# Sorting the second group's lists by one-hot matrix products, and layer 1's norm with ScalarE squares, in a two-layer sparse graph kernel

## The chip, the cores and the metric

One core of one Trainium2 chip runs the kernel. The metric is the device time of one execution in microseconds (us). The profile is of one execution; its engines are called PE (TensorE matmuls), PEld (TensorE weight loads), DVE (VectorE), ACT (ScalarE), POOL (GpSimd, which also issues the indirect DMAs) and SP (SyncE, which here only issues DMAs).

## The reference, cut to what matters

The input is x, 3327 x 512, and a sparse symmetric adjacency matrix adj with ones on its diagonal. Two residual layers follow each other:

```python
# layer 0: graph attention with 4 heads
feats  = einsum('nf,hfo->hno', x, W)
logits = leaky(e_self[:, :, None] + e_neigh[:, None, :], 0.2), -1e10 where adj == 0
out    = relu(softmax(logits) @ feats + b)
x      = layernorm(x + out)
# layer 1: two gated sums over the same neighbours
attn_a = sigmoid([adj @ x, x] @ Wa.T + ba);  attn_b likewise with Wb, bb
h      = x @ W_sa
e      = where(adj != 0, exp(-leaky(s_left[:, None] + s_right[None, :], 0.01)), 0)
x_a    = (e / (sum(e) + 1e-5)) @ h
x_b    = adj @ (x @ W_gcnb) + b_gcnb
x      = layernorm(x + sigmoid(attn_a * x_a + attn_b * x_b))
```

A row of adj has few ones, so both layers can be computed from lists of neighbours: a node's row of a table is fetched for each neighbour, weighted and summed.

## The kernel before, in words

Nodes are cut into 26 tiles of 128, in two groups: 12 tiles (the first group) and 14 (the second). The kernel runs in three stages, in an order written out by hand, and every engine executes its instructions in that order.

**Lists and features (0 to about 215 us).** adj is loaded in chunks; matmuls with powers of two (`make_codes`, L371) and the top-8 instructions of VectorE (`top8`, L69) turn each column into a list of neighbours. `features` (L344) makes the rows of `table0`. A node's list is a row of 32 words in the tile `st`: its number, 24 neighbours, its number within the group, and four scores. Within a group the nodes are then sorted by degree, so that a tile needs as many fetches as its longest list (`CAPS`, L26). `rank_b` (L464) computes each node's place in the order (`ranki`), and `sort` (L496) writes every tile's list rows to their places in DRAM by an indirect DMA (`scatter`, L143) and reads them back as `srt[g]`. The first group is sorted early, among the features; the second after the first three tiles' fetches have been issued (L809), on POOL's queue, with the reading back on SP's.

**Layer 0 (about 215 to 560 us).** A loop over the tiles (L828), in an order with long and short tiles mixed. `gather` (L592) fetches a tile's rows, one indirect DMA on POOL per neighbour slot, into buffers of up to 6 rows, of which there are 7 (`GB`); it is called three tiles ahead. `weigh_a` and `weigh_b` make the softmax weights on VectorE and ScalarE, `attend` (L748) scales the rows (two of three on VectorE, the third on ScalarE) and adds them up on TensorE by products with the identity. In iteration i the order on TensorE is: `columns2` of tile i-2 (needs a copy `xt` by ScalarE), the sums of tile i, the transposes of tile i-1 (`columns1`). VectorE's order is: the scaling of tile i, the residual sum and statistics of tile i-1, `columns3`, the weights of tile i+1. At i = 5 `climb(1, ...)` (L854) prepares the longest lists of the second group from `srt[1]`; the first fetch that needs `srt[1]` is of tile 23, called at i = 9. `publish` scales finished tiles and writes them to `table1`.

**Layer 1 (about 560 to 970 us).** A second loop (L1019) over the tiles: `gather` from `table1`; `weighted` (L958) makes the weighted sum on VectorE, one multiply-add (L967) per row; `plain_sum` (L973) makes the plain sum on TensorE, one product per row. To relieve TensorE, VectorE adds some rows in pairs (L969, chosen by `paired`, L937), and TensorE takes a pair as one row. `turn` transposes both sums, with copies on ScalarE, and `project` multiplies them with the two weight matrices. At the end of an iteration come L1059 (the residual sum of tile i-2), `weights_b` and `scaled_first` of the next tile (the latter one ScalarE instruction, L951, that starts the accumulator `sw`, which VectorE's first L967 needs), and `norm.add` with bn_stats and bn_aggr (L660, L661); at the end of each group of up to four tiles the same call also makes the inverse root (L669 to L676).

Of the kernel before, what the change touches and what calls it, by code (L numbers as in the profile page):

```python
# [8 lines left out]
F32 = mybir.dt.float32  # L9
AF = mybir.ActivationFunctionType  # L10
# [69 lines left out]
def sparse_pass(  # L80
# [59 lines left out]
    own1 = dram.tile([NG[1] * P, 2, ROW], F32, name="own1")  # L140
    lists = [dram.tile([n * P, LW], I32, name=f"lists{i}") for i, n in enumerate(NG)]

# [47 lines left out]


    p0 = tc.alloc_tile_pool(name="p0", bufs=1, side="right")
    psl = tc.alloc_tile_pool(name="psl", bufs=1, space=PSUM, side="right")
# [80 lines left out]
    nc.gpsimd.memset(all1, 1.0)  # L274
    st = p0.tile([P, NT, LW], I32, name="st")
    nc.gpsimd.memset(st, 0)
    nc.gpsimd.iota(st[:, :, 0], pattern=[[P, NT]], base=0, channel_multiplier=1)
    for g, n in enumerate(NG):
        nc.gpsimd.iota(st[:, T0[g] : T0[g] + n, S + 1], pattern=[[P, n]], base=0, channel_multiplier=1)

# [63 lines left out]
    def features(t):  # L344

        i = t * P // CH
        xc = xcs[i]
        o = t * P - chunks[i]
        pf = psf.tile([P, 2, 512], F32, tag="pf", name=f"pf{t}")
        for k, hh in ((k, hh) for hh in range(2) for k in range(KT)):  # L350
            nc.tensor.matmul(  # L351
                pf[:, hh, :HC], xc[:, k, o : o + P], w0[:, k, hh, :], start=(k == 0), stop=(k == KT - 1)
            )
        row = pj.tile([P, ROW], F32, tag="row", name=f"row{t}", bufs=4)
        nc.scalar.copy(row[:, 0:F].rearrange("p (h o) -> p h o", h=2), pf[:, :, 0 : F // 2])
        nc.scalar.activation(
            row[:, F : F + H], pf[:, 0, F // 2 : HC], AF.Identity, bias=pad if t == NT - 1 else 0.0
        )
        nc.scalar.copy(row[:, F + H : ROW], st[:, t, 0:1].to_broadcast([P, H]))
        nc.scalar.copy(st[:, t, S + 2 : S + 2 + H].bitcast(F32), pf[:, 1, F // 2 : HC])  # L360
        nc.gpsimd.dma_start(table0[t * P : (t + 1) * P, :], row)  # L361
# [65 lines left out]
    def pick(i):  # L427
# [21 lines left out]
        )  # L449
        nc.vector.tensor_scalar(st[:, t0 : t0 + nt, 1 : S + 1], some[:, :nt], float(N), None, ALU.add)  # L450

# [12 lines left out]
    def rank_b(g):  # L464
# [19 lines left out]
        ranks[g] = rk  # L484
        return ranki

# [8 lines left out]

    def sort(g, ranki, queue):  # L496

        put = lambda t: scatter(f"lists{g}", lists[g][:, :], ranki[:, t : t + 1], st[:, T0[g] + t, :])
        tasks.extend(lambda t=t: put(t) for t in range(NG[g]))
        tasks.append(lambda: queue.dma_start(srt[g], lists[g].rearrange("(t p) w -> p t w", p=P)))  # L500
        if g == 0:
            tasks.extend(lambda j=j: own_x(j) for j in range(NG[0]))

# [55 lines left out]
    for i in range(len(chunks)):  # L559
        make_codes(i)  # L560
        more(1)
        if i == NC0:
            rankis[0] = rank_b(0)
            sort(0, rankis[0], nc.gpsimd)
        turn_codes(i)
# [22 lines left out]
    gp = ctx.enter_context(tc.tile_pool(name="gp", bufs=1))  # L588
    m0 = ctx.enter_context(tc.tile_pool(name="m0", bufs=2))
    ps = ctx.enter_context(tc.tile_pool(name="ps", bufs=1, space=PSUM))  # L590
# [88 lines left out]
    class Norm:  # L679
# [6 lines left out]
        def add(self, k, y):  # L686
# [7 lines left out]
            done = (self.first, *rsqrt(self.pool, self.mv, n, f"{self.tag}{k}"))  # L694
            self.first, self.mv = k + 1, None
            return done

# [109 lines left out]
    for i in range(AHEAD):  # L807
        got[order0[i]] = gather(table0, order0[i])
    sort(1, rankis[1], nc.sync)  # L809
    later(len(tasks))  # L810
    nc.sync.dma_start(own1[:, 0, :], xo)
# [16 lines left out]
    for i in range(NT + 3):  # L828
# [22 lines left out]
        if 2 <= i < NT + 2:  # L851
            columns3(order0[i - 2])
        if i == 5:
            climb(1, m0, psx.tile([P, B * H], F32, tag="pcol", name="climb1", bufs=2)[:, : B + H])  # L854
# [10 lines left out]
    covered()  # L865
    psx.release()


# [68 lines left out]
    def paired(j):  # L937

        left = 4 + (CAPS[j] >= 13)
        got_ = set()  # L940
        for s0, n, g, _ in got[j]:
            for i in range(0, n - 1, 2):
                if left:
                    got_.add(s0 + i)
                    left -= 1
        return got_
# [62 lines left out]
    ends = {3, 7, 11, 15, 19, 22, 24, 25}  # L1009
    norm = Norm(m1, "n1", ends)  # L1010
    at_ = lambda i: order[i] if 0 <= i < NT else None
# [5 lines left out]
    scaled_first(at_(0))  # L1017
    ready = None
    for i in range(NT + 3):  # L1019
# [5 lines left out]
        if jp is not None:  # L1025
            sp = zs[jp, "sp"] = m1.tile([P, F], F32, tag="sp", name=f"sp{jp}")
            nc.scalar.activation(sp, plain[jp], AF.Copy, scale=gates[jp][:, 1:2])
            turn(jp, 0)
            turn(jp, 1)
        if j is not None:  # L1030
            plain_sum(j, False)
            weighted(j, 0)
        if jpp is not None:
            za = zs[jpp] = m1.tile([P, F], F32, tag="za", name=f"za{jpp}", bufs=GRP + 3)
# [22 lines left out]
        if jpp is not None:  # L1057
            za = zs[jpp]
            nc.vector.scalar_tensor_tensor(za, za, 0.5, row1(jpp)[:, 0:F], ALU.mult, ALU.add)  # L1059
        if j1 is not None:  # L1060
            weights_b(j1)
            scaled_first(j1)
        if jpp is not None:
            ready = norm.add(i - 2, zs[jpp])

# [451 lines left out]
```

## Time and profile before

| | |
|---|---|
| median of 3 runs | 970.43 us (966.85 to 974.26) |
| the profiled execution | 971.21 us, of which the span of the core is 969.50 us |
| mean granted TensorE clock | 0.907 of full |
| busy: PE, DVE, ACT, POOL | 804.4, 716.6, 278.2, 626.2 us |
| fetches of rows (L615) on POOL | 464, mean 1033 ns, 479.2 us busy |
| layer 0's sums (L763) on PE | 504 instructions, 230.8 us |
| layer 1's multiply-adds (L967) on DVE | 226, mean 749 ns, 169.3 us |
| layer 1's pair sums (L969) on DVE | 95, mean 692 ns, 65.7 us |
| scatters of lists (L145) | 26, median 971 ns, the second group's between 216 and 235 us |

An engine's busy time is a sum over stages with different limits. A group's "idle before" is time in which that engine stood still, with the instruction or transfer that ended the wait. A product of 32-bit numbers is two instructions on PE; their durations overlap, so a run of n such instructions in one line of the timeline gives the true rate: 24 of 128x512 took 10.46 us at full clock, 0.43 us each. POOL shows about 0.30 us of "issue" between two indirect DMAs even when it waits for nothing.

### The profile page before, as it was taken

The page shows a single profiled execution, that of the slowest core. Times are in us where ns is not written, and L with a number is a line of the kernel's source. Part 1 is how long each engine was busy: PE and PEld are TensorE (multiplying, and loading weights), DVE is VectorE, ACT ScalarE, POOL GpSimd, SP SyncE. Part 2 cuts the span into 40 slices and gives each one's busy share as a digit, 9 for nine tenths or more (in the row PEclk, how much of TensorE's full clock was granted, in tenths as well). Part 3 has the DMA queues.
Part 4 walks back from the last instruction along what each step waited for, and adds up shares of the span by engine and source line. Part 5 has one row for each costly group of instructions (what it writes and reads, how often), then busy time and mean ns, then how long its engine had stood idle before and what let it go on. Part 6 is the DMA issues. An engine that isn't in the chain of part 4 may idle for free.

```text
span 969.5 us, 10086 instructions
## 1 busy us (share of the span) xinstructions
PE 804.4 (83%) x2534; PEld 421.7 (43%) x2534; DVE 716.6 (74%) x2118; ACT 278.2 (29%) x820; POOL 626.2 (65%) x664
## 2 busy tenths in 40 slices
PE   4399887338897998989979839998989989899893
PEld 3277675114344444444434514444434434344341
DVE  4277878886465676667756738799989989989873
ACT  1022211004234343435333403223222232232231
POOL 6611144777777777677777367777777777777411
PEclk9699998557898999989998958999989999999997
DMA  9799999972988787787777257776676776666400
GB/s 321 289 353 376 399 332 382 360 205 76 401 312 247 218 271 225 257 282 231 231 227 232 92 166 192 195 187 188 189 197 196 187 195 183 187 185 188 129 33 36
DMA packets 74242, 221.87 MB, mean 229 GB/s; under 512 B 14944, under 2 KB 19216, under 8 KB 73280
## 3 DMA queue, kind: packets, MB, share of 16 engines
q0 software_dynamic: 47008, 153.87, 53.7%
q1 hardware_dynamic: 24512, 65.17, 17.7%
q10 hardware_dynamic: 2656, 2.10, 0.7%
q8 instruction: 23, 0.38, 0.2%
q14 instruction: 43, 0.35, 0.1%
HBM read 200.01 MB, written 28.55 MB: 236 GB/s over the span
## 4 chain that ended last, share of the span: by engine, by line
PE 45%; DVE 19%; DMA 12%; POOL 11%; issue 7%; ACT 4%; DVEq 0%; ACTq 0%; POOLq 0%
PE acc L763 21%; PE pf L351 9%; POOL g L615 7%; DMA g<-table,srt 7%; DVE sw L967 7%; DMA at<-in_adjB 3%; PE po L1007 3%; PE pcol L787 3%; PE acc L988 3%; PE acc L752 3%; DVE g L969 2%; ACT xt L784 1%; DMA a_row<-in_a_self 1%; PE x1t L780 1%; POOL sprod L321 1%
## 5 line engine op out<-in xcount | busy, mean ns | idle before, releaser
L615 POOL DMA_INDIRECT g<-table,srt x464 | 479.2, 1033 | 147.9 <-issue 121.9
L763 PE MATMUL acc<-g,ident 128*128 128x512 f32 x504 | 230.8, 614 | 1.4 <-DVE g L760 1.4
L967 DVE SCALAR_TENSOR_TENSOR sw<-g,e,sw 128x512 f32<-128x512 f32 x226 | 169.3, 749 | 12.7 <-ACT sw L951 8.5
L763 PEld LDWEIGHTS acc<-g,ident 128*128 128x128 f32 x504 | 100.4, 199 | 132.1 <-issue 101.1
L988 PE MATMUL acc<-g,ident 128*128 128x512 f32 x262 | 128.6, 618 | 24.9 <-DVE g L969 14.7
L351 PE MATMUL pf<-w,xc 128*128 128x260 f32 x416 | 102.2, 408 | 13.3 <-DVE w L291 13.3
L760 DVE TENSOR_TENSOR g<-g,w 128x512 f32<-128x512 f32 x176 | 110.5, 695 | 0.6
L1007 PE MATMUL po<-wg,sT 128*128 128x512 f32 x208 | 98.0, 616 | 0.0
L351 PEld LDWEIGHTS pf<-w,xc 128*128 128x128 f32 x416 | 83.6, 204 | 29.2 <-DVE w L291 14.1
L1007 PE MATMUL po<-wsa,sT 128*128 128x512 f32 x208 | 95.2, 601 | 0.3 <-ACT sT L1000 0.3
L758 ACT ACTIVATE g<-g,w 128x128 f32<-128x128 f32 x304 | 91.6, 389 | 0.7 <-DVE w L743 0.7
L988 PEld LDWEIGHTS acc<-g,ident 128*128 128x128 f32 x262 | 49.1, 193 | 95.8 <-issue 44.7
L361 POOL DMA_DIRECT2D table<-row x26 | 14.4, 555 | 85.4 <-ACT st L360 85.4
L969 DVE TENSOR_TENSOR g<-g 128x512 f32<-128x512 f32 x95 | 65.7, 692 | 3.3
L1037 ACT ACTIVATE za<-za 128x512 f32<-128x512 f32 x26 | 16.4, 631 | 170.8 <-DVE za L1035 170.8
L1007 PEld LDWEIGHTS po<-wg,sT 128*128 128x128 f32 x208 | 41.4, 200 | 52.2 <-issue 52.0
L1007 PEld LDWEIGHTS po<-wsa,sT 128*128 128x128 f32 x208 | 40.2, 194 | 51.3 <-issue 48.9
L145 POOL DMA_INDIRECT out<-za,srt x26 | 29.1, 1118 | 50.1 <-ACT za L1052 44.0
L787 PE MATMUL pcol<-v,xt 128*128 128x8 f32 x208 | 32.4, 283 | 33.1 <-ACT xt L784 33.1
L379 PE MATMUL pc<-at,pow 128*32 128x512 bf16 (+1 forms) x182 | 24.3, 436 | 33.2 <-DMA at<-in_adjB 19.4
L787 PEld LDWEIGHTS pcol<-v,xt 128*128 128x128 f32 x208 | 30.0, 222 | 38.8 <-ACT xt L784 38.6
L717 DVE TENSOR_TENSOR w<-g,srt 128x20 f32<-128x20 f32 (+3 forms) x55 | 9.7, 184 | 48.2 <-DMA g<-table,srt 46.9
(236 smaller groups left out, 933.3 us busy)
## 6 DMA issues: line engine op xcount, KB each, us to landing
at<-in_adjB SPq DMA_DIRECT2D x78, 512.0 KB, 11.4
g<-table,srt POOLq DMA_INDIRECT x464, 3.8
table<-row POOLq DMA_DIRECT2D x26, 260.0 KB, 6.2
xc<-in_xB SPq DMA_DIRECT2D x6, 1024.0 KB, 7.1
own<-in_xo SPq DMA_DIRECT2D x1, 3640.0 KB, 23.5
own<-table SPq DMA_DIRECT2D x1, 3640.0 KB, 42.0
at<-in_adjL SPq DMA_DIRECT2D x13, 256.0 KB, 13.2
table<-x1a SPq DMA_DIRECT2D x12, 260.0 KB, 5.7
```

Source lines behind the costliest of these rows:

```text
L145: put = nc.gpsimd.indirect_dma_start(out=dst, out_offset=bass.IndirectOffsetOnAxis(ap=rows, axis=0), in_=src, in_offset=None, bounds_check ...
L351: nc.tensor.matmul(pf[:, hh, :HC], xc[:, k, o : o + P], w0[:, k, hh, :], start=(k == 0), stop=(k == KT - 1))
L615: nc.gpsimd.indirect_dma_start(out=buf[:, q - q0, :], out_offset=None, in_=table[:, :], in_offset=bass.IndirectOffsetOnAxis(ap=srt[g][:, i ...
L752: nc.tensor.matmul(acc, ident, bias0, start=True, stop=False)
L758: nc.scalar.activation(gv[:, h, :], gv[:, h, :], AF.Copy, scale=w[:, s, h : h + 1])
L760: nc.vector.tensor_tensor(gv, gv, w[:, s, :].rearrange("p (h o) -> p h o", o=1).to_broadcast([P, H, FO]), ALU.mult)
L763: nc.tensor.matmul(acc, ident, buf[:, o + s - s0, 0:F], start=False, stop=(s == CAPS[j] and j not in T0))
L787: nc.tensor.matmul(pcol, xt1[:, k, :], v1[:, k, :], start=(k == 0), stop=(k == KT - 1))
L967: nc.vector.scalar_tensor_tensor(sw, g[:, i, 0:F], e[:, s : s + 1], sw, ALU.mult, ALU.add)
L969: nc.vector.tensor_add(g[:, i, 0:F], g[:, i - 1, 0:F], g[:, i, 0:F])
L988: nc.tensor.matmul(plain[j], to, row, start=(not sums_of_two and i == 0), stop=(sums_of_two and i == len(rows) - 1),)
L1007: nc.tensor.matmul(proj[j], sT[:, k, :], wt[:, k, :], start=(half + k == 0), stop=(half + k == KT))
```

## The change

1. `sort` is split. The first group is sorted as before (`sort0`). The second group's 14 scatters and the reading back are gone. In their place `sort1`, called at the end of iterations i = 1 to 7 of layer 0 for two tiles of lists each, makes two VectorE instructions per tile (`row_is`, 128 x 128, and `spread`, 128 x 14 x 30) and one product on TensorE that adds into one PSUM tile; after the last one, two VectorE copies take it to `srt[1]`. `row_is` and `spread` have two buffers each. `rank_b(1)` gets four more small VectorE instructions that split the place into tile and row. `climb(1, ...)` moves from i = 5 to i = 8.
2. The constants on POOL change: the list tile is split into `st0` and `st1` (the second in 32-bit floats), and a few index rows are added.
3. In layer 1 `Norm` is replaced by `SquareNorm`: L1059 gets an accumulator output with the row's sum, one small VectorE instruction makes the negative mean, and ScalarE squares the row with that as its bias, with the sum of squares as an accumulator output. The inverse root is made in the next iteration, after `weighted(j, 0)`.
4. `turn(jp, 1)` comes after `plain_sum(j, False)`.
5. `paired` takes up to five pairs of a tile's rows (six for the longest tiles), where it took four (five).
6. The pool `m0` is released ahead of layer 1.

```diff
-        nc.vector.tensor_scalar(st[:, t0 : t0 + nt, 1 : S + 1], some[:, :nt], float(N), None, ALU.add)
+        nc.vector.tensor_scalar(
+            (st0, st1)[g][:, l0 : l0 + nt, 1 : S + 1], some[:, :nt], float(N), None, ALU.add
+        )
...
+        ti = p0.tile([P, NM], I32, name="ti")
+        nc.vector.tensor_scalar(ti[:, :n], ranki[:, :n], 7, None, ALU.logical_shift_right)
+        nc.vector.tensor_scalar(ranki[:, :n], ranki[:, :n], P - 1, None, ALU.bitwise_and)
+        to = ls.tile([P, 2, NM], F32, name="to")
+        nc.vector.tensor_copy(to[:, 0, :n], ti[:, :n])
+        nc.vector.tensor_copy(to[:, 1, :n], ranki[:, :n])
+        return to
...
+    def sort1(to, t0, t1):
+        n = NG[1]
+        if t0 == 0:
+            in_place.append(ps.tile([P, KT * P], F32, tag="pt", name="sorted1")[:, : n * W1])
+        for t in range(t0, t1):
+            row_is = ls.tile([P, P], F32, tag="row_is", name=f"row_is{t}", bufs=2)
+            nc.vector.tensor_scalar(row_is, columns, to[:, 1, t : t + 1], None, ALU.is_equal)
+            spread = ls.tile([P, n, W1], F32, tag="spread", name=f"spread{t}", bufs=2)
+            nc.vector.scalar_tensor_tensor(
+                spread, tiles_.to_broadcast([P, n, W1]), to[:, 0, t : t + 1],
+                st1[:, t : t + 1, :].to_broadcast([P, n, W1]), ALU.is_equal, ALU.mult,
+            )
+            nc.tensor.matmul(
+                in_place[0], row_is, spread.rearrange("p t w -> p (t w)"), start=(t == 0), stop=(t == n - 1)
+            )
+        if t1 == n:
+            by_tile = in_place[0].rearrange("p (t w) -> p t w", t=n)
+            nc.vector.tensor_copy(srt[1][:, :, : S + 2], by_tile[:, :, : S + 2])
+            nc.vector.tensor_copy(srt[1][:, :, S + 2 : W1].bitcast(F32), by_tile[:, :, S + 2 :])
...
+    class SquareNorm:
...
+        def add(self, k, y):
+            i = k - self.first
+            less_mean = self.of[:, 0, i : i + 1]
+            nc.vector.tensor_scalar(less_mean, less_mean, -1.0 / F, None, ALU.mult)
+            square = self.pool.tile([P, F], BF16, tag="square", name=f"square{self.tag}{k}", bufs=1)
+            nc.scalar.activation(square, y, AF.Square, bias=less_mean, accum_out=self.of[:, 1, i : i + 1])
+            return k in self.ends
...
-    sort(1, rankis[1], nc.sync)
-    later(len(tasks))
...
-        if i == 5:
+        if 0 < i <= 7:
+            sort1(rankis[1], 2 * i - 2, 2 * i)
+        if i == 8:
             climb(1, m0, psx.tile([P, B * H], F32, tag="pcol", name="climb1", bufs=2)[:, : B + H])
...
-        left = 4 + (CAPS[j] >= 13)
+        left = 5 + (CAPS[j] >= 13)
...
             turn(jp, 0)
+        if j is not None:
+            plain_sum(j, False)
+        if jp is not None:
             turn(jp, 1)
         if j is not None:
-            plain_sum(j, False)
             weighted(j, 0)
+        if full:
+            ready = norm.finish(i - 3)
...
-            nc.vector.scalar_tensor_tensor(za, za, 0.5, row1(jpp)[:, 0:F], ALU.mult, ALU.add)
+            nc.vector.scalar_tensor_tensor(
+                za, za, 0.5, row1(jpp)[:, 0:F], ALU.mult, ALU.add, accum_out=norm.total(i - 2)
+            )
...
-        if jpp is not None:
-            ready = norm.add(i - 2, zs[jpp])
+        full = jpp is not None and norm.add(i - 2, zs[jpp])
```

`SquareNorm.finish` makes the same chain of small instructions as L669 to L676, from the sums of squares.

## The prediction, made before the changed kernel was run

> **What bounds the kernel now.** I read the windows view first, one row per stage, its columns being the window, the busy time and count of PE, PEld, DVE, ACT and POOL, then granted PE clock, DMA share and GB/s:
>
> ```profile
> 300.00:350.00 50.00, 42.05 (x128) 21.63 (x127) 35.29 (x109) 22.18 (x73) 38.12 (x40) 0.93 0.79 231
> 850.00:900.00 50.00, 49.74 (x140) 23.53 (x139) 46.58 (x107) 13.35 (x33) 39.34 (x35) 1.00 0.67 188
> ```
>
> In layer 0 PE is busiest, and POOL is full too: 40 instructions with 0.30 us of issue each make 38.1 + 12 = 50 us. In layer 1 PE, DVE and POOL all look full. So the timeline of each must say who waits for whom. POOL first, around the second group's sort:
>
> ```profile
> 214.99 0.95 POOL L624 DMA_INDIRECT g<-table,ids  x1 [0.30 <-DVE v1sum L823]
> 216.25 1.00 POOL L145 DMA_INDIRECT lists<-st,ranki  x1 [0.30 <-DVE w L729]
> ...
> 233.99 0.97 POOL L145 DMA_INDIRECT lists<-st,ranki  x1 [0.30 <-DVE w L729]
> 235.26 0.99 POOL L615 DMA_INDIRECT g<-table,srt  x1 [0.30 <-issue]
> ```
>
> The wrong line to trust would be the releaser's name: every gap is 0.30, so POOL waits for nothing. The 14 scatters hold the fetches of the fourth tile (i = 3) back from 216.25 to 235.26: 19.0 us. Who pays is seen on PE:
>
> ```profile
> 254.27 0.60 PE L780 MATMUL x1t<-ident,x1a 128*128 128x128 f32 x4
> ...
> 259.58 1.88 PE L787 MATMUL pcol<-v,xt 128*128 128x8 f32 x8 [4.71 <-ACT xt L784]
> ...
> 277.06 1.06 PE L787 MATMUL pcol<-v,xt 128*128 128x8 f32 x8 [0.73 <-ACT xt L784]
> ...
> 302.28 0.29 PE L547 MATMUL climb<-of,to_row 128*128 128x14 f32 x2
> 308.33 1.87 PE L787 MATMUL pcol<-v,xt 128*128 128x8 f32 x8 [5.76 <-ACT xt L784]
> ```
>
> A normal tile has a gap of 0.73 us ahead of L787. Two are long: 4.71 (DVE waited for the fourth tile's fetch, and ScalarE's copy stood behind those weights) and 5.76 (DVE sat 9.50 us in front of `climb` at i = 5; then weights, four publishes of 2.92 us together on ScalarE, and only then the copy). After both the same eight products take 1.87 instead of 1.06. From 312 to 404 PE has no other gap over 0.73 but one of 2.50, while a tile's last fetch lands 12 us or so ahead of its sum (at i = 9 POOL ends at 329.8, 3.8 us to landing by the page, the sum begins at 347.3): PE bounds, POOL doesn't. From 395 POOL bounds, but its restart at 395.15, after a wait of 4.25, comes when L843 (394.20 to 394.88) has read the own rows out of a buffer, and L843 follows PE. So PE's position near i = 13 sets the end of layer 0.
>
> In layer 1 the waits view of DVE from 640 to 925 lists three waits, 11.0 us in all, one of them this:
>
> ```profile
> DVE sw L967 <- ACT sw L951: 5.9, 7, 1.7
> ```
>
> DVE is never idle for PE's sums, and only 1.3 us for a fetch. It bounds, until short tiles leave PE alone on the chain from 919 to 954. The end of an iteration on DVE and ACT:
>
> ```profile
> 818.24 0.52 DVE L932 TENSOR_SCALAR e<-e,gate 128x11 f32<-128x11 f32 x1
> 818.44 0.69 DVE L660 BATCH_NORM_STATS2 st<-za 128x6 f32<-128x512 f32 x1
> 819.16 0.18 DVE L661 BATCH_NORM_AGGREGATE mvn<-st 128x2 f32<-128x6 f32 x1
> 819.55 1.54 DVE L967 SCALAR_TENSOR_TENSOR sw<-g,e,sw 128x512 f32<-128x512 f32 x2 [0.20 <-ACT sw L951]
> ...
> 818.79 0.72 ACT L951 ACTIVATE sw<-x1b,e 128x512 f32<-128x512 f32 x1 [1.22 <-DVE e L932]
> ```
>
> The statistics lie between L932 and L967, exactly where DVE must wait for L951 anyway (818.79 + 0.72 = 819.51). At the iteration's end before this one it is the same: L951 ends at 806.83, L967 starts at 806.87.
>
> **What the Trainium skill says.** "TensorE: Matmul & The Clock Gate", Part 1 (the HAM clock gate): about an idle window of 3.4 us halves PE's clock, and about as much work restores it. The trace agrees: 1.88 against 1.06 after gaps of 3.39 us and more. "VectorE: DVE Perf Modes", "Two Vector instructions with no wait between them": an operation with an accumulator output is two instructions. DVE has none in this trace; ScalarE's read of its accumulator at L909 takes 0.19 us. "Vector Engine (DVE) Microarchitecture Reference", section 7: a scalar-tensor-tensor with two SBUF sources that aren't bf16 halves its throughput, with no port left for the accumulator's readback. Without an accumulator the trace contradicts a halving: L1059 has such sources and takes 0.68, as L843 does from PSUM.
>
> **The change, part by part.**
>
> *Constants and features.* POOL ends its constants at 4.7 and waits 6.29 for a transfer; a few index rows more (0.13 to 0.38 each) fit there. The features' ScalarE copies keep their size. 0.
>
> *Rank.* Four more DVE instructions at 0.2 each (as L483 with its gap) between L483 and the first weights: on the path, +0.8.
>
> *The 14 scatters and SP's reading.* POOL -19.0, but limited by seven buffers: the fourth tile's second buffer is free only when tile 11's sum ends (225.1). Even so its 13 fetches at 1.26 end near 236 (eight of them after 226), and later ones stay ahead of PE. SP's two `own1` copies, which stood behind the reading back at 236.49, go early, beside the lists stage; the three tiles fetched there land 8 us or more ahead of use (third tile: 219.2, used 227.3). 0 but for the gap that goes.
>
> *The products of `sort1`.* 128x420: 0.43 x 420/512 = 0.35 an instruction, two a product, two products: 1.4 us of PE per iteration, seven times. From i = 2 to 6 they cover the 0.73 gap: net 0.7. Their DVE work, per tile 0.2 (as L437's 96 elements, 0.18) and 0.6 (L458: 0.52 for 350, with 1.05 ns an element from there to 512), 1.7 an iteration with gaps, lies where DVE is ahead of PE; 0. Two buffers each let DVE wait for the products before last, done by then.
>
> *The two hand-overs.* At i = 7 the copies to `srt[1]` wait for PE's last product, and weights, ScalarE's exp, casts and the copy `xt` queue behind them, PE behind that: 0.5 (L474: 350 from PSUM in 0.52) + 0.2 + 1.1 of weights + 0.24 + 0.4 + 0.56 = 3.0, with latency 3.1. At i = 8 `climb` does it again without the publishes: 5.76 - 2.92 = 2.9. The fetch that needs `srt[1]` (tile 23) waits for a buffer until the sum of i = 8 in any case.
>
> Ledger of PE until i = 9, in us: rank +0.8; i = 1: +1.4; i = 2: -4.71 - 3.1 (clock: 0.82 on L787, 0.95 on L752, 12.53 instead of 11.2 on the sum) + 1.4 = -6.4; i = 3, 4, 6: +2.1; i = 5: -5.76 - 2.7 (clock likewise) - 0.29 + 1.4 = -7.35; i = 7: +1.4 + 3.1 - 0.73 = +3.8; i = 8: +0.29 + 2.9 - 0.73 = +2.45. Sum -3.2, before the clock. The gap of 2.50 at 386.70 cost 1.5 (14.41 for 30 instructions, 12.9 at full clock), that of 3.39 at 416.76 cost 3.1. Between them I take 2.4 for each new gap: **layer 0 +1.6**, bounds -3.2 (none) and +3.0 (3.1 each).
>
> *ScalarE's squares.* Removed: 0.87 of DVE per tile, hidden behind L951: 0, except at one of the longest tiles, where L967 waits for L661 (-0.7). Added on DVE: the accumulator's read in L1059, ahead of L932, on the path. Likeliest 0.15, between 0.06 and ScalarE's 0.19; upper bound L1059 at half rate, +0.53. From i = 6 to 23 DVE bounds: 18 x 0.15 = +2.7. Before i = 6 fetches bound (DVE waited 4.83 for one at 626.5). `less_mean` (0.16) hides behind L951. The square comes after L951 on ScalarE, some 0.9 with its read; behind it queue `sp` and both copies of `turn`. Moving `turn(jp, 1)` behind at least one row (0.86 on PE) covers `sp`; project's wait stays about 0. The inverse root keeps its 2.3 us of DVE, elsewhere. End: square, read and `less_mean` (about 1.3) for 0.92 of statistics: +0.5.
>
> *Fifth pair.* By the list lengths only five tiles (lengths 11, 11, 12, 14, 14) have one more pair. DVE +0.65 each: +3.2. PE -0.86 each, not bounding there: 0.
>
> *`m0`'s release.* The next pool waits for readers done by 561.5; its first use that matters waits for a fetch until 573. 0.
>
> **Layer 1: +2.7 + 3.2 - 0.7 + 0.5 = +5.7.** Total +7.3 against the profiled run's own 971.2: 978.5. The median of runs lies 0.8 below that run, so I say **978**.
>
> **Rivals.** *Slow accumulator:* L1059 at half rate. One mechanism at one place, +0.53 in place of 0.15 in 18 iterations, +6.8, and 0.4 at the end: 985; with both clocks cold 986. For it: the skill's sentence. Against: L1059's 0.68 now. It decides from L1059 over about 0.95 us. *DVE relieved:* if L951's cover were not the limit, 18 x 0.65 = 11.7 would go (0.87 less `less_mean`), and with the clock warm (layer 0 at -3.2) the time is 971.2 - 3.2 + 5.7 - 11.7 - 0.8 = 961; if a hand-over is hidden too, 958. The 806.83 and 806.87 speak against it. *Table loads:* if the square belonged to another table set, two loads of 1.28 (row L355) per tile would stand in front of L951's successors, 26 x 2.6 = 66 us, hidden in part: 1000 or more. Unlikely. *POOL was the bound:* 19 us off, 952; the landings 12 us ahead of use exclude most of it.
>
> **How the numbers follow.** About 1% (9.7 us) is what a measurement can tell from no change. The likeliest case has 0.6: its own range is 970 to 984, and the part over 980.1, with what queues behind the new waits and isn't priced, is 0.2. The slow accumulator 0.2, DVE relieved or POOL's bound 0.15 (0.1 under 960.7), table loads and the rest 0.05, slower. So faster 0.10, same 0.45, slower 0.45. The range 966 to 990 leaves out most of the relieved case and table loads.
>
> **What would show it.** Gap ahead of L787's like near 255 gone, and a third fetch buffer's wait on PE in its place; two gaps of about 3 us at i = 7 and 8, with the eight products at 1.9 after them if the clock fell; L967 still starting 0.04 after ScalarE's `sw`, DVE idle 0.5 ahead of it; L1059 and its read under 0.9; 100 pair sums. Wrong if L967 starts earlier after L932 than now, or PE has no gaps at i = 7 and 8.

## The result, and the profile after

| | before | after |
|---|---|---|
| median of 12 runs each | 970.5 us (966.85 to 974.26) | 969.3 us (967.27 to 976.42) |
| ratio, 95% interval | | 0.9997 (0.9981 to 1.0013) |
| the profiled execution, its span | 971.21, 969.5 us | 967.27, 965.2 us |
| busy: PE, DVE, ACT, POOL | 804.4, 716.6, 278.2, 626.2 us | 800.9, 712.6, 297.7, 611.7 us |

No difference can be measured, where 978 was forecast. Here and below, a ratio and its interval leave out runs more than 1.5% above the fastest of the same kernel, while a median takes in all runs. The two windows shown of before read so after the change (window, busy time and count of PE, PEld, DVE, ACT and POOL, granted PE clock, DMA share, GB/s):

```profile
300.00:350.00 50.00, 44.40 (x126) 21.76 (x125) 30.94 (x101) 18.31 (x59) 32.78 (x34) 0.93 0.69 197
850.00:900.00 50.00, 47.47 (x127) 21.36 (x126) 45.73 (x105) 12.82 (x34) 39.05 (x36) 1.00 0.68 190
```

The stages differ in place by a few us, so these lines give only the picture: POOL is no longer full in this stretch of layer 0 (32.8 us and 34 times 0.30 of issue make 43), and nothing looks relieved in layer 1. The timelines say more. POOL, where the scatters were:

```profile
214.56 0.95 POOL L676 DMA_INDIRECT g<-table,ids  x1 [0.30 <-issue]
215.82 0.95 POOL L667 DMA_INDIRECT g<-table,srt  x1 [0.30 <-issue]
...
225.97 0.95 POOL L667 DMA_INDIRECT g<-table,srt  x1 [3.83 <-PE acc L855]
...
235.06 0.95 POOL L667 DMA_INDIRECT g<-table,srt  x1 [0.30 <-issue]
```

The fourth tile's fetches start at 215.82, 19.4 us earlier. After five of them POOL waits 3.83 us for PE to free a buffer, which the prediction had said, and the eighth after that ends at 236.0. PE, near the first place where it had stood still, and at the two new ones:

```profile
255.11 1.58 PE L548 MATMUL sorted<-spread,row_is 128*128 128x420 f32 x4
256.52 0.95 PE L879 MATMUL pcol<-v,xt 128*128 128x8 f32 x8
...
321.18 1.58 PE L548 MATMUL sorted<-spread,row_is 128*128 128x420 f32 x4
325.48 1.06 PE L879 MATMUL pcol<-v,xt 128*128 128x8 f32 x8 [2.72 <-ACT xt L876]
...
327.34 9.59 PE L855 MATMUL acc<-g,ident 128*128 128x512 f32 x18
...
337.19 0.29 PE L599 MATMUL climb<-of,to_row 128*128 128x14 f32 x2
340.36 1.11 PE L879 MATMUL pcol<-v,xt 128*128 128x8 f32 x8 [2.88 <-ACT xt L876]
```

At 256.52 there is no gap where 4.71 was: the fourth tile's fetches no longer come late, and the sort's products (1.4 us) fill what a normal tile has left, 0.73. At the ends of iterations i = 7 and 8, ahead of the next tile's products, are the two gaps that were forecast at 3.1 and 2.9. DVE stands in front of both hand-overs:

```profile
322.80 0.54 DVE L553 CAST srt<-sorted 128x364 int32<-128x364 f32 x1 [9.71 <-PE sorted L548]
...
337.52 0.17 DVE L600 TENSOR_TENSOR of<-climb,step_of 128x10 f32<-128x10 f32 x1 [3.75 <-PE climb L599]
```

In layer 1, the end of an iteration on DVE, then on ACT:

```profile
813.53 0.68 DVE L1156 SCALAR_TENSOR_TENSOR za<-za,x1b 128x512 f32<-128x512 f32 x1
814.14 0.08 DVE L1156 DVE_READ_ACCUMULATOR za<-za,x1b 128x1 f32 x1
814.14 0.15 DVE L1022 TENSOR_SCALAR gate<-gate 128x1 f32<-128x1 f32 x1
...
814.52 0.51 DVE L1025 TENSOR_SCALAR e<-e,gate 128x11 f32<-128x11 f32 x1
814.72 0.31 DVE L768 TENSOR_SCALAR ofn<-ofn 128x1 f32<-128x1 f32 x1
815.82 1.54 DVE L1060 SCALAR_TENSOR_TENSOR sw<-g,e,sw 128x512 f32<-128x512 f32 x2 [0.79 <-ACT sw L1044]
```

```profile
815.06 0.72 ACT L1044 ACTIVATE sw<-x1b,e 128x512 f32<-128x512 f32 x1 [1.21 <-DVE ofn L768]
815.69 0.71 ACT L770 ACTIVATE squaren<-za,ofn 128x512 bf16<-128x512 f32 x1
816.30 0.19 ACT L770 ACTIVATION_READ_ACCUMULATOR squaren<-za,ofn 128x1 f32 x1
816.40 0.17 ACT L984 COPY e<-x1a 128x1 f32<-128x1 f32 x1
```

And the same instruction without accumulator, on DVE in the kernel before:

```profile
817.26 0.68 DVE L1059 SCALAR_TENSOR_TENSOR za<-za,x1b 128x512 f32<-128x512 f32 x1
817.86 0.14 DVE L929 TENSOR_SCALAR gate<-gate 128x1 f32<-128x1 f32 x1
```

From its start to the next instruction's: 0.61 us with the accumulator, 0.60 without. The read of 0.08 overlaps. DVE's 0.87 of statistics are gone, and it now stands 0.79 idle in front of the first multiply-add, which starts 0.04 after ScalarE's `sw` (815.06 + 0.72), as before. DVE's waits from 637 to 917 show the same as a sum (us, times, longest), where before has 5.9 us in 7 waits in the same window:

```profile
DVE sw L1060 <- ACT sw L1044: 19.0, 18, 2.4
```

### The profile page after: what moved, and what is told of

Same layout as the page of the kernel before. It is cut to its first block, busy times and chain, and to the rows that moved or that the text cites. A ratio compares the mean times of both kernels' runs of the same rounds, so it can differ in the third digit from the quotient of the medians.

```text
span 965.2 us, 10206 instructions
## 1 busy us (share of the span) xinstructions
PE 800.9 (83%) x2552; PEld 418.7 (43%) x2552; DVE 712.6 (74%) x2157; ACT 297.7 (31%) x872; POOL 611.7 (63%) x654
## 4 chain that ended last, share of the span: by engine, by line
PE 58%; DVE 12%; DMA 11%; POOL 10%; issue 5%; ACT 4%; DVEq 0%; ACTq 0%; POOLq 0%
PE acc L855 20%; PE po L1100 11%; PE pf L369 9%; PE acc L1081 7%; POOL g L667 7%; DMA g<-table,srt 6%; DVE sw L1060 4%; DMA at<-in_adjB 3%; PE pcol L879 3%; PE acc L844 3%; DVE g L1062 2%; PE pt L1091 2%; ACT za L1149 1%; DMA a_row<-in_a_self 1%; ACT xt L876 1%
## 5 line engine op out<-in xcount | busy, mean ns | idle before, releaser
L855 PE MATMUL acc<-g,ident 128*128 128x512 f32 x504 | 230.1, 613 | 1.6 <-DVE g L852 1.6
L855 PEld LDWEIGHTS acc<-g,ident 128*128 128x128 f32 x504 | 99.8, 198 | 131.1 <-issue 99.5
L1081 PE MATMUL acc<-g,ident 128*128 128x512 f32 x252 | 123.2, 615 | 21.9 <-DVE g L1062 12.1
L1100 PE MATMUL po<-wg,sT 128*128 128x512 f32 x208 | 94.5, 597 | 0.0
L1081 PEld LDWEIGHTS acc<-g,ident 128*128 128x128 f32 x252 | 47.3, 194 | 90.3 <-issue 41.1
L1062 DVE TENSOR_TENSOR g<-g 128x512 f32<-128x512 f32 x100 | 69.2, 692 | 3.5
L397 PE MATMUL pc<-at,pow 128*32 128x512 bf16 (+1 forms) x182 | 24.4, 438 | 32.7 <-DMA at<-in_adjB 19.4
L879 PE MATMUL pcol<-v,xt 128*128 128x8 f32 x208 | 29.5, 269 | 25.1 <-ACT xt L876 25.1
L1093 ACT COPY sT<-pt 128x512 f32<-128x512 f32 x52 | 30.2, 582 | 55.3 <-PE pt L1091 55.1
L876 ACT COPY xt<-x1t 128x512 f32<-128x512 f32 x26 | 15.2, 583 | 97.8 <-PE x1t L872 97.8
## 6 DMA issues: line engine op xcount, KB each, us to landing
own<-in_xo SPq DMA_DIRECT2D x1, 3640.0 KB, 33.9
```

The costliest lines, as they stand in the source:

```text
L855: nc.tensor.matmul(acc, ident, buf[:, o + s - s0, 0:F], start=False, stop=(s == CAPS[j] and j not in T0))
L879: nc.tensor.matmul(pcol, xt1[:, k, :], v1[:, k, :], start=(k == 0), stop=(k == KT - 1))
L1062: nc.vector.tensor_add(g[:, i, 0:F], g[:, i - 1, 0:F], g[:, i, 0:F])
L1081: nc.tensor.matmul(plain[j], to, row, start=(not sums_of_two and i == 0), stop=(sums_of_two and i == len(rows) - 1),)
L1093: nc.scalar.copy(sT, pt)
L1100: nc.tensor.matmul(proj[j], sT[:, k, :], wt[:, k, :], start=(half + k == 0), stop=(half + k == KT))
```

## The experiments

To compare single executions, four stretches are used, all from the timelines:

- **A** runs from POOL's first fetch to the end of PE's sum of i = 7.
- **B** runs on to the end of the sum of i = 9.
- **C** runs on to the end of the last sum of layer 0.
- **D** lies in layer 1. It runs from the end of DVE's wait for a fetch near 623 to the end of its wait for `po` (PE's projection) near 942; in old_turn_3 that is the one that ends at 948.78.

The ends of D in before, in after and in four_pairs, on DVE:

```profile
626.52 0.23 DVE L902 TENSOR_SCALAR e<-g,x1b 128x3 f32<-128x3 f32 x1 [4.83 <-DMA g<-table,srt]
945.53 0.75 DVE L1035 SCALAR_TENSOR_TENSOR za<-bias_g,gate,po 128x512 f32<-128x512 f32 x1 [4.35 <-PE po L1007]
```

```profile
623.12 0.23 DVE L995 TENSOR_SCALAR e<-g,x1b 128x3 f32<-128x3 f32 x1 [3.27 <-DMA g<-table,srt]
941.93 0.75 DVE L1132 SCALAR_TENSOR_TENSOR za<-bias_g,gate,po 128x512 f32<-128x512 f32 x1 [5.14 <-PE po L1100]
```

```profile
625.64 0.23 DVE L995 TENSOR_SCALAR e<-g,x1b 128x3 f32<-128x3 f32 x1 [5.03 <-DMA g<-table,srt]
942.26 0.75 DVE L1132 SCALAR_TENSOR_TENSOR za<-bias_g,gate,po 128x512 f32<-128x512 f32 x1 [4.78 <-PE po L1100]
```

From D is taken what one wait, that of a tile with long lists for `to_rows`, has over 0.9 us. It is 3.2 us in before and 0.9 in sort_only, whose layer 1 is the same code. The eight products in front of it on PE say why. They took 5.99 us in before and 3.68 in sort_only, and that is the whole difference: PE ran slower there in one execution than in the other (3.68 in five of the ten executions below, 5.38 to 6.53 in before, old_turn_3, late_copies, both_3 and both_four).

```profile
722.13 5.99 PE L1007 MATMUL po<-wg,sT 128*128 128x512 f32 x8
```

```profile
722.68 3.68 PE L1100 MATMUL po<-wg,sT 128*128 128x512 f32 x8
```

Without this correction D is 319.0 in before, 321.8 in old_turn_3, and 320.6, 315.8 and 313.1 in late_copies, both_3 and both_four; in the others it changes nothing. All in us:

| kernel | A | B | C | D | time, ratio to before |
|---|---|---|---|---|---|
| before | 154.5 | 21.8 | 197.4 | 316.7 | |
| after | 141.9 | 30.9 | 197.8 | 318.8 | 0.9997 (0.9981 to 1.0013) |
| sort_only | 141.8 | 33.9 | 198.2 | 316.6 | 968.3; 0.9989 (0.9969 to 1.0010) |
| l1_only | 152.6 | 21.8 | 198.0 | 318.8 | 972.5; 1.0033 (1.0015 to 1.0051) |
| four_pairs | 143.6 | 30.9 | 197.5 | 316.6 | 967.0; 0.9990 (0.9970 to 1.0010) |
| late_copies | 141.9 | 22.8 | 199.1 | 318.0 | 961.4; 0.9925 (0.9905 to 0.9945) |
| bn_norm_3 | 142.6 | 33.9 | 199.1 | 318.3 | one execution, 974.3 |
| old_turn_3 | 143.1 | 30.9 | 197.8 | 320.3 | one execution, 974.1 |
| both_3 | 146.3 | 22.8 | 199.0 | 312.5 | 957.7; 0.9885 (0.9861 to 0.9909) |
| both_four | 142.4 | 24.5 | 197.8 | 310.3 | 955.6; 0.9862 (0.9837 to 0.9887) |

The four kernels from sort_only to late_copies ran on one chip, where the kernel before took 969.0 (median); both_3 and both_four on another, where it took 968.3; bn_norm_3 and old_turn_3 on a third, with 972.7 in one execution. What lies outside the four stretches doesn't differ by kernel, but it scatters: POOL's first fetch comes between 178.6 and 182.2 us in these ten executions, and from C's end to D's start are 72.7 to 74.2 us.

### sort_only and l1_only: each half of the change alone

sort_only is after with this taken back in layer 1 (and the order of the transposes with it); l1_only is before with it put in (cut; the accumulator output and `finish` go with `Norm` and `SquareNorm`):

```diff
-        left = 5 + (CAPS[j] >= 13)
+        left = 4 + (CAPS[j] >= 13)
-    norm = SquareNorm(m1, "n1", ends)
+    norm = Norm(m1, "n1", ends)
```

> After, with the statistics, the order of the transposes and the four pairs of the kernel before in layer 1: only the second group's lists and their products are changed. Theory A (the two new gaps of 2.7 and 2.9 us on PE cost 1.9 each in clock, not 2.4, and the gap that goes at i = 2 takes a colder stretch with it): PE ends the sum of i = 9 some 3 us earlier than before, layer 0 ends 2.5 to 3.5 earlier, and the time is 967 to 968 us (-3). Theory B (the prediction's ledger of layer 0 holds, and something else offsets it): layer 0 +1.6, 972 us. Theory C (the two kernels' profiled executions differ by chance): layer 0 within 1 us of before, 970.

> Before, with layer 1 of the kernel after (squares on ScalarE, fifth pair, order of the transposes). Theory A (the accumulator's read is free, 0.01 an iteration; the fifth pair costs 0.5 to 0.8 on each of five tiles; about as much comes back at tiles where DVE waited for PE's rows): from the start of layer 1's fetches to PE's last sum within 1 us of before (377.9 us), the time 969 to 971. Theory B (the prediction's terms hold in a layer 1 that starts as before): layer 1 +5.7, the time 976. Theory C (all of the profiled gain is layer 1's): 967.

No theory has both of its numbers right. The lists' half took 968.3 against 969.0, nothing that can be told from zero; the layer's half was slower by 0.33%, 3.2 us, with an interval from 1.5 to 4.9. Layer 0 as a whole (A, B and C) has 373.9 in sort_only and 373.7 in before, which is theory C's "within 1 us". Its A is as short as after's, but B is 3.0 us longer, with the same code. PE's timeline of sort_only says why:

```profile
327.15 1.88 PE L879 MATMUL pcol<-v,xt 128*128 128x8 f32 x8 [2.72 <-ACT xt L876]
...
343.35 1.72 PE L879 MATMUL pcol<-v,xt 128*128 128x8 f32 x8 [2.88 <-ACT xt L876]
...
346.77 9.69 PE L855 MATMUL acc<-g,ident 128*128 128x512 f32 x18
```

The gaps are 2.72 and 2.88 to the digit as in after, but here the eight products take 1.88 and 1.72 where after had 1.06 and 1.11, and the second sum 9.69 where after had 8.62. The same gap costs one execution more clock than another. So a single profile doesn't settle layer 0 to better than 3 us.

### four_pairs, bn_norm and old_turn: the three parts of layer 1

four_pairs is after with one line undone:

```diff
-        left = 5 + (CAPS[j] >= 13)
+        left = 4 + (CAPS[j] >= 13)
```

> After with four pairs of rows (five for tiles of 13 and more) as before: 95 pair sums for 100, and PE has one product more on each of five tiles. Theory A1 (DVE bounds on those tiles, and each pair's 0.65 us is on the path): layer 1 shorter by 2.5 to 3.3 us than in after, time -3. Theory A2 (PE bounds there as much as DVE, since DVE then waits for PE's rows): layer 1 within 1 us of after or longer by up to 4 us (five products of 0.86).

D is 316.6 against 318.8: the five pairs cost 2.2 us in all, 0.44 each of the 0.65 that DVE spends on one. (The same code scatters by less: 318.8, 318.8 and 318.0 in after, l1_only and late_copies, 316.7 and 316.6 in before and sort_only.) By D theory A1 comes nearest, a little below its range; the time, 967.0, doesn't contradict it. With four pairs, D is what it is in before and sort_only (316.7 and 316.6). So the squares and the order of the transposes together cost nothing and bring nothing that D can show.

Whether they cancel was asked of two more kernels, each after with one thing undone (bn_norm is cut as above):

```diff
# bn_norm
-    norm = SquareNorm(m1, "n1", ends)
+    norm = Norm(m1, "n1", ends)
# old_turn
-        if j is not None:
-            plain_sum(j, False)
-        if jp is not None:
             turn(jp, 1)
         if j is not None:
+            plain_sum(j, False)
             weighted(j, 0)
```

> The kernel of bn_norm once more, one look, for a chip without the long waits. From DVE's wait for a fetch near 623 to its wait for PE's last projection but one (less what the tile-0 wait for `to_rows` has over 0.9 us): theory A (the accumulator's read is free and the statistics lie in the wait for `sw`) 318.8 plus or minus 0.6 as after; prediction's terms 316.8; rival 'DVE relieved' up to 330.

> The kernel of old_turn once more, one look. The same stretch: theory B (the move is worth nothing) 318.8 plus or minus 0.6; theory A (ScalarE's `sp`, now behind the square, is waited for longer by the transposes) 319.5 to 322.

bn_norm_3 has 318.3: without the squares layer 1 is at most 0.5 shorter, no more than the scatter. Theory A holds, and the rival "DVE relieved" falls: 0.87 us a tile of DVE's work went and nothing came of it. DVE's waits from 555 to 965 in bn_norm_3 (us, times, longest), then those of after in its layer 1 (561.1 to 928.1):

```profile
DVE sw L1060 <- ACT sw L1044: 8.7, 11, 1.7
```

```profile
DVE sw L1060 <- ACT sw L1044: 25.1, 26, 2.4
```

old_turn_3 has 320.3, 1.5 more than after and within its theory A (319.5 to 322). PE's waits in the same two windows, old_turn_3 first:

```profile
PE pt L1091 <- ACT sp L1120: 15.6, 9, 4.4
```

```profile
PE pt L1091 <- ACT sp L1120: 6.9, 4, 2.5
```

The square stands in front of `sp` on ScalarE, and in the old order PE's transposes wait for that; the new order takes away most of this wait, not all (before, without squares, has 2.4 us in 3 waits). That it makes the square free is what these numbers suggest. But bn_norm_3 and old_turn_3 are single executions, and 1.5 is one difference between two executions, about twice the scatter of the same code.

### late_copies: the hand-overs

```diff
@@ sort1: the two copies to srt[1] become a function of their own, sorted_out()
-        if i == 8:
-            climb(1, ...)
...
             weigh_b(order0[i + 1])
+        if i == 7:
+            sorted_out()
+        if i == 8:
+            climb(1, ...)
```

> After with one thing moved: the two copies out of PSUM at i = 7 and the second group's `climb` at i = 8 are issued behind the weights of the following tile, so that no weights queue behind DVE's wait for PE. Theory A (the two gaps of 2.72 and 2.88 us and about 1.9 us of clock after each are the price of the hand-overs): PE has no gap over 0.8 at i = 7 and 8, the sum of i = 9 ends 8 to 9.5 us earlier than in after, and what is left at the end of layer 0 is 4 to 9. Time 960 to 965. Rival (POOL bounds layer 0 once PE is relieved): the sum of i = 9 ends 8 us earlier, but PE waits for fetches before i = 13 and layer 0 ends within 2 us of after: 967 to 969.

The time fell by 0.75% against before (interval 0.55 to 0.95%), to 961.4. PE's timeline of late_copies at i = 7 and 8:

```profile
322.20 0.95 PE L881 MATMUL pcol<-v,xt 128*128 128x8 f32 x8
...
323.96 7.89 PE L857 MATMUL acc<-g,ident 128*128 128x512 f32 x18
...
333.36 0.39 PE L601 MATMUL climb<-of,to_row 128*128 128x14 f32 x2 [1.08 <-DVE of L600]
333.61 1.04 PE L881 MATMUL pcol<-v,xt 128*128 128x8 f32 x8
```

Theory A holds, but for a gap over 0.8: there is no gap ahead of the products, one of 1.08 ahead of `climb`, and 18 instructions of the sum take 7.89 where after needed 9.59. B is 22.8 in place of 30.9, and nothing of the 8.1 is lost before the end of layer 0 but 1.3 (C). The rival, POOL as the next bound, falls. The two hand-overs were a price that a later place in DVE's order doesn't pay, since the first fetch that needs `srt[1]` is called at i = 9.

### weights_first, both and both_four: is it the wait for `sw`?

weights_first moves one instruction of after, both adds late_copies to it, and both_four takes four pairs:

```diff
         if jpp is not None:
             za = zs[jpp]
+            if j1 is not None:
+                weights_b(j1)
+                scaled_first(j1)
             nc.vector.scalar_tensor_tensor(
                 za, za, 0.5, row1(jpp)[:, 0:F], ALU.mult, ALU.add, accum_out=norm.total(i - 2)
             )
-        if j1 is not None:
+        elif j1 is not None:
             weights_b(j1)
             scaled_first(j1)
```

> After with one thing moved in layer 1: L1156 (0.6 us, the residual with its accumulator) is issued behind the weights of the next tile, so that it fills DVE's wait for ScalarE's `sw` (0.73 to 0.79 us in every iteration of after). Theory A (DVE sets the pace of the iterations): the wait falls to about 0.15, 0.6 us go in each of 18 iterations, layer 1 from the fetch that ends DVE's wait near 623 to PE's last projection takes 308 us in place of 318.8, time 957 to 960. Theory B (PE is as full: 98% busy there; DVE sets the pace only on the long tiles): DVE's gain turns up as waits on PE's rows or `po`, layer 1 is 1 to 4 us shorter, time 964 to 967. Theory C (square and `less_mean` come later on ScalarE and DVE, and the next iteration's `sp` and turn wait for them): no gain, 968 to 970.

> After with the moves of late_copies and weights_first together. If layer 0 and layer 1 are independent, as their fetches' barrier between them suggests, the gains add: -7.3 measured for late_copies against before, and what weights_first shows: 951 to 960. If not, no better than late_copies, 961.

> After with layer 1's statistics on DVE again (two instructions of 0.69 and 0.18 us a tile, no accumulator, no squares on ScalarE) and five pairs. Theory A (the statistics lie in DVE's wait for `sw`, the accumulator's read is free): from DVE's fetch wait near 623 to PE's last projection 318.8 plus or minus 0.6 us, as after; DVE's waits for `sw` fall from 25 us to about 9. Prediction's terms: 2.0 us shorter than after (the accumulator's read 2.7, less 0.7). Rival 'DVE relieved': up to 11 us longer.

> After with the second half of the transposes (`turn(jp, 1)`) issued ahead of the next tile's first rows, as before. Theory A (PE is full, and the first half's transposes wait for the square in front of `sp` on ScalarE in either order): PE's waits for `sp` grow from 6.9 us to 8 to 12 us, and layer 1 is 0 to 3 us longer. Theory B (the move is worth nothing): within 0.6 us of after's 318.8. If the order had cost time: shorter than 318.8.

These four ran on one more chip, and again on the next:

> The kernel of weights_first, on another chip: there the kernel before took 1099 us, with waits for transfers of up to 40 us in layer 0 that are in no trace of the first chip. Expected as before: theory A (DVE sets the pace): DVE's wait for `sw` falls to about 0.15 an iteration, from DVE's fetch wait near 623 to its wait for PE's last projection but one 308 us in place of 318.8, time 957 to 960. Theory B (PE as full, DVE sets the pace on long tiles only): 1 to 4 us shorter, 964 to 967. Theory C (square and `less_mean` come later and the next turn waits for them): 968 to 970.

> The kernel of both, on another chip. If the gains of layer 0 and layer 1 add: 951 to 960. If not: 961, as late_copies.

> The kernel of bn_norm, on another chip. Theory A (statistics lie in DVE's wait for `sw`, the accumulator's read is free): 318.8 plus or minus 0.6 us from DVE's fetch wait near 623 to its wait for PE's last projection but one, as after; waits for `sw` 9 us in place of 25. Prediction's terms: 2.0 us shorter than after. Rival 'DVE relieved': up to 11 us longer.

> The kernel of old_turn, on another chip. Theory A: PE's waits for `sp` grow from 6.9 us to 8 to 12, the same stretch is 0 to 3 us longer than after's 318.8. Theory B (the move is worth nothing): within 0.6 us. If the order had cost time: shorter.

| kernel | first of these chips: time, ratio | second (_2): time, ratio |
|---|---|---|
| before | 1098.9 | 1112.4 |
| weights_first | 1100.9; 0.9995 (0.9954 to 1.0036) | 1115.8; 0.9963 (0.9917 to 1.0009) |
| both | 1099.6, no ratio | 1103.5; 0.9965 (0.9924 to 1.0006) |
| bn_norm | 1101.1; 1.0003 (0.9964 to 1.0042) | 1109.1; 0.9943 (0.9907 to 0.9978) |
| old_turn | 1098.5; 0.9962 (0.9920 to 1.0004) | 1117.1; 1.0001 (0.9952 to 1.0050) |

None of the expected times came out, since before itself was slower by 14%: engines stood still there for which the trace shows no reason. ScalarE in weights_first waited twice for over 9 us, with no releaser on the core for the first wait and, for the second, products on PE that had ended 1.3 us before:

```profile
685.79 0.58 ACT L1093 COPY sT<-pt 128x512 f32<-128x512 f32 x1 [9.73 <-remote]
...
695.61 0.58 ACT L1093 COPY sT<-pt 128x512 f32<-128x512 f32 x1 [9.24 <-PE acc L1081]
```

The intervals are some 0.4% to either side, as wide as what was asked, and the one ratio away from 1, bn_norm_2's, is not borne out by the first chip's: nothing is concluded from these eight, and why the two chips are slower stays open. both and both_four then ran on a chip on which before took 968.3:

> late_copies and weights_first together, on a chip where the kernel before takes about 970. If the gains of layer 0 and layer 1 add: late_copies' -7.3 and, from the stretches of weights_first without an engine's long wait (57.3 to 57.6 us from one publish to the next in place of after's 58.8 to 59.8), 1.5 to 2 more in each of some four such stretches: 952 to 957. If PE or POOL takes the place of DVE: 961 as late_copies.

> both with four pairs of rows. Theory A (the fifth pair costs DVE 0.65 us and some 0.45 net on five long tiles, whichever order the end of the iteration has): 1.5 to 2.5 us less than both. Rival (with DVE relieved by the order, PE's five products more are on the path): equal or up to 4 us more than both.

both_3 is 957.7, 0.40% below late_copies by the two ratios, just above the expected 952 to 957; its D is 312.5 in place of 318.0. DVE in both_3 at the end of an iteration:

```profile
869.55 0.38 DVE L1029 TENSOR_SCALAR e<-e,gate 128x11 f32<-128x11 f32 x1
869.75 0.69 DVE L1163 SCALAR_TENSOR_TENSOR za<-za,x1a 128x512 f32<-128x512 f32 x1
870.36 0.08 DVE L1163 DVE_READ_ACCUMULATOR za<-za,x1a 128x1 f32 x1
870.48 0.15 DVE L770 TENSOR_SCALAR ofn<-ofn 128x1 f32<-128x1 f32 x1
870.72 1.56 DVE L1064 SCALAR_TENSOR_TENSOR sw<-g,e,sw 128x512 f32<-128x512 f32 x2
```

The idle 0.79 is gone: the instruction that used to lie ahead of the weights fills it. DVE's waits for `sw` from 553 to 945 in both_3:

```profile
DVE sw L1064 <- ACT sw L1048: 9.4, 9, 2.1
```

So the wait for `sw` is what ate the squares' gain, and 5.5 us of it come back (4.8 without the correction of D). That is more than the 1 to 4 of theory B of weights_first and half of theory A's 0.6 x 18 = 10.8; that on the other tiles something else than DVE sets the pace is likely, but no run shows it. The A of this execution, both_3's slowest (962.4), is some 4 us longer than late_copies' with the same code up to there, which stays open. both_four is another 2.2 shorter in D (2.6 without the correction), as four_pairs was against after and as its theory A had it, and its time ratio, 0.9862, is the lowest; the step from both_3 (0.23%) is within the two intervals. It is 1.4% below before, some 13 us, and about as much below after, whose ratio is 0.9997.

## Why the prediction was wrong, and where it was right

The forecast was +7.3 on the profiled execution, 978 as a median; the measured median is 969.3. The two halves of the forecast and their terms, against the means of the executions with the same code (layer 0: before and l1_only, against after, sort_only, four_pairs, bn_norm_3 and old_turn_3):

| term, as the prediction put it | forecast | measured |
|---|---|---|
| rank, on the path | +0.8 | 0.0: PE's first sum ends 46.9 us after POOL's first fetch in both (means; single executions 46.2 to 47.5) |
| i = 1 and i = 2 (gap and clock go, products come) | -5.0 | -4.7 (before and l1_only differ by 3.3) |
| i = 3 to 6 | -5.25 | -6.3 |
| i = 7 and 8, with 2.4 of clock for each gap | +11.05 | +10.3 (+9.1 three times, +12.1 twice) |
| from i = 9 on | 0 | +0.4 |
| **layer 0** | **+1.6** | **-0.3** |
| accumulator's read, less 0.7 at a long tile | +2.0 | at most +0.5 |
| fifth pair | +3.2 | +2.2 |
| end | +0.5 | not seen: D's end to the span's end 22.8 to 24.0 with the old norm, 23.2 to 24.4 with the new |
| **layer 1** | **+5.7** | **+2.2** |

**The step that failed** is the price of the accumulator's read: "Likeliest 0.15, between 0.06 and ScalarE's 0.19 ... 18 x 0.15 = +2.7". It measured 0.01 from start to start, 0.2 us in 18 iterations, since the read overlaps with the instruction after it. The prediction had taken a second instruction as a serial one. ScalarE's read, from whose 0.19 the upper end of that came, shows the same error: in the lines above it starts at 816.30 and lasts 0.19, but the next instruction starts at 816.40, when the square ends. What counts is how much later the next instruction starts, not how long the row is. What "VectorE: DVE Perf Modes" says in "Two Vector instructions with no wait between them" is right, the trace now shows the second instruction; that it costs time doesn't follow. The slow accumulator fell with it: section 7 of the "Vector Engine (DVE) Microarchitecture Reference" would have the rate halved, and L1156 takes 0.68 with the accumulator as L1059 without. It is the largest single step, but not the whole. Of the 5.4 us by which the terms' sum (+7.3) lies above that of the stages (+1.9), it makes up to 2.0, the small terms of layer 0 together 1.9, the fifth pair 1.0 and the end 0.5.

**The fifth pair** was mis-sized in the same direction: 0.65 each was DVE's work, and 0.44 is what the layer became longer. PE has one product fewer on those tiles, which the prediction put at nothing; that this gives back the difference is likely, but no run shows it.

**Layer 0** was right in its mechanisms, with most of its small terms on the dear side: a sort product costs 0.4 net where it fills a gap, not 0.7 (the sum of i = 4 ends 13.9 us after that of i = 3 in after, 13.5 in before), and the rank can't be told from nothing. The sum comes out 1.9 lower. The clock's price of a gap was well bounded (none to 3.1): without it the two hand-overs are 6.25, so that after paid 1.4 for each and sort_only 2.9. Part 1 of "TensorE: Matmul & The Clock Gate" (the HAM clock gate) speaks of an idle window of about 3.4 us; gaps of 2.72 and 2.88 were enough in sort_only for products at 1.88 and 1.72 in place of 1.06, while after a gap of 2.71 in l1_only they took 1.06. It also says that the window runs freely, whatever the kernel does; that could be why the same gaps cost 1.4 in one execution and 2.9 in another, but no run here was made to test it.

**Right**: that the scatters' gap goes and PE, not POOL, is what the seven buffers wait for; both new gaps, their places, their cause (DVE in front of the hand-over, ScalarE's copy behind it) and their sizes; that the statistics lay in the wait for `sw`, so that their going brings nothing; that 100 pair sums cost DVE time. In part right: that the order of the transposes covers `sp`, for 6.9 us of PE's waits were left; they cost D nothing that shows (four_pairs has 6.6 us of them and before's D). A slip in a rival: 0.87 less `less_mean` (0.16) is 0.71, not 0.65, and "DVE relieved" would have been 12.8 in place of 11.7.

The stages add up to +1.9, and sort_only and l1_only, timed, to +2.1 (give or take 2.6); after itself, timed, is -0.3 (-1.8 to +1.3). These overlap. Whether the halves help each other by a us or two was not settled.

**What to make of "no change".** By the stages it is two prices that cancel against two gains, not four edits without effect. Gains: the two stalls of before, the scatters' and that of `climb` at i = 5, -11.0 (i = 1 to 6). Prices: the two hand-overs, +10.3, and the fifth pair, +2.2. The statistics' going brought nothing, since a wait took their place. late_copies shows that the price of the hand-overs was avoidable, four_pairs and both_four show, by D, the same for the fifth pair, and both_3 shows that the hole left by the statistics could be used.

## What to carry to other kernels

When an engine's work is taken away, look at what the next instruction on it waits for: if that was ready no earlier than the work's end, the work was free, and the gain comes only when something that is on the path is moved into the hole. When a result is handed from one engine to another in a hand-written order, put the reading instruction behind everything that somebody else waits for; two hand-overs with gaps of 3 us ate here (10.3 with the clock) what the end of two stalls had brought (11.0). Price a second instruction by the start of the one that follows it, not by its own duration.

## What the hardware showed that was not expected

An accumulator output on a VectorE scalar-tensor-tensor of 128x512 costs 0.01 us here: 0.68 with it and 0.68 without, its read of 0.08 hidden. The TensorE clock after the same gaps of 2.72 and 2.88 us differed from one execution to the next by 3.0 us of PE time in total. Over 50 runs of before the time and the mean granted clock go together, 4.2 us for 0.01 of clock (correlation -0.56, so about a third of the variance of a spread from 963.2 to 974.7; which of the two makes the other isn't shown). With 14 to 20 runs against these 50 an interval is still some 0.2% to either side. The stall of the code before worked as a buffer: PE began layer 0 4.2 us later in l1_only than in before (first sum done at 229.3 and 225.1), the gap that is 4.71 in before was 2.71 in l1_only, and at the end of the sum of i = 3 0.8 were left. And on two of the chips every kernel took some 14% longer, with engines idle for up to 9.7 us between instructions in the lines shown, and no cause found.
